# Where the operands of the rounded float32 products begin: large constants first in their pool, small tiles filled up

## The chip, the cores and the metric

The kernel runs on one core of a Trainium2 chip. The metric is the device time of one execution in microseconds (us): the median over several runs of the same program. TensorE (PE in the profile) does the matrix products, VectorE (DVE) and ScalarE (ACT) the elementwise work, GpSimd (POOL) a few small operations, and SyncE (SP) issues nearly all loads from device memory (HBM). Data are held in SBUF, 128 partitions with a byte address inside each; products land in PSUM, 8 banks per partition.

## The reference

Two layers, each an attention part and a feed-forward part, with a residual sum and a layer norm after each part. All inputs are float32. `x` is 2 x 512 tokens of width 512.

```python
x = layernorm(x + L0_attn(x))   # linear attention on a stored memory M, z; 8 key/value heads of 128
x = layernorm(x + L0_ffn(x))    # ternary weights; values truncated to int8 after up and after down
x = layernorm(x + L1_attn(x))   # one head of 128, softmax over 512 keys
x = layernorm(x + L1_ffn(x))    # silu(x Wg) * (x Wu), then Wd; inner width 1376
```

The inner width of both feed-forward parts is 1376: ten chunks of 128 and one of 96.

## The kernel before, in words

**Two kinds of product.** A full float32 product is one call in the program and two matmul records in the trace. A product of two tiles of type `float32r` (called rounded float32 here: the tile is written already rounded) is one record. The two attention parts use full float32: queries (line 334), the read of the memory (379), query/key (778), value (791), scores (806), attention times values (863), output (880). The two feed-forward parts use rounded products. Layer 0 up (line 539) multiplies ternary weights `tu` with a high and a low part of the rows, `xh` and `xl`, 352 products; layer 0 down (595) has 88. Layer 1 splits rows and weights each into three rounded parts and forms three products for each product of the reference: up (977) has 528, down (1052) has 231 of 512 columns and 66 of 256. In each product one tile is loaded into the array (the stationary operand, 128 or 96 columns a partition) and the other streams through (the moving operand, 512 columns, 256 in the 66).

**Order of the work.** The two batches `b` are worked side by side, in four stages: layer 0 attention, layer 0 feed-forward, layer 1 attention, layer 1 feed-forward. The order on each engine is that of the program, with some operations tied behind others by name; POOL's order is the written one alone. Loads go out on SP's queue in the written order, all weights of layer 0 first; those of layer 1 wait for the buffers of layer 0.

**Memory.** Tiles come from pools that lie one behind the other in each partition. Inside a pool the tags follow in the order of their first use, and each tile takes its bytes per partition rounded up to 32. The first pool, `const`, begins at byte 16512, which is 129 x 128. Its tags in order are `bq`, `z`, `ident`, four single columns, `ones`, `wqkv`, `bqk`, `bv`, `wo1`, `bo`, and small tables and flags. Then follow `wffn` (up weights, tags `gu0` to `gu10`), `xp` (the rows), `xtp` (two transposed row blocks, tag `xt`), `small` (columns of statistics, among them `col`, four buffers), `wop` (six pairs of rows, tag `wo`), `wqp` (four, tag `wq`), and the pools of the stages.

The space is used again under other names. The layer 0 high parts `xh` are `xt` tiles; the low parts `xl` are `wo` tiles; the ternary up weights `tu` are `wq` tiles; the ternary down weights `td` lie in `gu` tiles (line 583). In layer 1 the row parts of batch 0 (`r0_0` to `r0_5`, line 898) are `wo` tiles; those of batch 1 are two `xt` and two `wq` tiles (lines 902, 903). Weight parts take whatever units are free: `it_early` (stage pool), `ugu` (in `gu` tiles, line 746), `uwd` (in tiles of the down weights), `u_wqkv`, `u_wo1` and `u_bo` (in `const`, lines 1081 to 1083).

Where the pools and the operand tiles begin, as the rest of the byte address over 128:

| Place | Operands of rounded products there | Rest over 128 |
|---|---|---|
| `const`: wqkv | `u_wqkv` | 64 |
| `const`: wo1, bo | `u_wo1`, `u_bo` | 96 |
| `wffn` | `td`, `ugu` | 64 |
| `xtp` | `xh`, two tiles of the batch 1 row parts | 64 |
| `wop` | `xl`, row parts of batch 0 | 0 |
| `wqp` | `tu`, two tiles of the batch 1 row parts | 0 |
| stage pools | `it_f`, `it_early`, `uwd` | 0 |

By place, 369 of the 1199 products of 512 columns have both operands at a rest of 0. In 382 only the moving operand is at 64, in 257 only the stationary one; in 145 both are at 64; the other 46 have one at 96.

**Other places that the change touches.** The start: POOL builds the identity `ident` (line 86), DVE fills `ones` (96), and eight products of `ones` (101) run before the first transposes. `fold(h)` (line 363): one product, a column `c` of tag `col` written by ACT and read by ACT in the next operation; it is called for h = 0 and 1, 2 and 3, 4, 5 and 6, 7 at five points of the query loop.

Of the kernel before, what the change touches and what calls it, by code (L numbers as in the profile page):

```python
# [10 lines left out]
F32 = mybir.dt.float32  # L11
# [8 lines left out]
P = 128  # L20
B, S, HID = 2, 512, 512
NT = S // P
NK = HID // P
NH, G, D = 8, 4, 128
# [12 lines left out]
def kernel(  # L37
# [19 lines left out]
    nc = tc.nc  # L57
# [3 lines left out]
    const = ctx.enter_context(tc.tile_pool(name="const", bufs=1))  # L61
# [3 lines left out]
    small = ctx.enter_context(tc.tile_pool(name="small", bufs=4))  # L65
    ps = ctx.enter_context(tc.tile_pool(name="ps", bufs=8, space=PSUM))

    def psum(name):
        return ps.tile([P, 512], F32, tag="mm", name=name)

# [11 lines left out]
    bq = const.tile([D, NH], F32, tag="bq", name="bq")  # L82
    z = const.tile([D, NH], F32, tag="z", name="z")

    ident = const.tile([P, P], F32, tag="ident", name="ident")
    make_identity(nc, ident)
    ln_eps = const.tile([P, 1], F32, tag="ln_eps", name="ln_eps")
    nc.vector.memset(ln_eps, LN_EPS)
# [3 lines left out]
    nc.vector.memset(den_eps, DEN_EPS)  # L92
    below_half = const.tile([P, 1], F32, tag="below_half", name="below_half")
    nc.vector.memset(below_half, -BELOW_HALF)
    ones = const.tile([P, P], F32, tag="ones", name="ones")
    nc.vector.memset(ones, 1.0)


    rise = psum("rise")
    for _ in range(8):  # L100
        nc.tensor.matmul(rise[:, :P], ones, ones, start=True, stop=True)
# [4 lines left out]
    def transposed(rows, name, cuts=0):  # L106


        xt = xtp.tile([P, NK, S], F32, tag="xt", name=f"xt_{name}")
        pts = {}  # L110

        def turn(k, t, i=0):
            if (k, i) not in pts:
                pts[k, i] = psum(f"pt_{name}_{k}_{i}")
            nc.tensor.transpose(pts[k, i][:, ts(t, P)], rows[t][:, ts(k, P)], ident)

        def copy(k, at, i=0):
            move = nc.vector.tensor_copy if k % 2 else nc.scalar.copy
            copies.append(move(xt[:, k, at], pts[k, i][:, at]))

        if cuts:
            for i in range(cuts):
                for t in range(i * NT // cuts, (i + 1) * NT // cuts):
                    for k in range(NK):
                        turn(k, t, i)
                for k in range(NK):
                    copy(k, ts(i, S // cuts), i)
        else:
            for k in range(NK):
                for t in range(NT):  # L130
                    turn(k, t)
                copy(k, slice(0, S))
        return xt
# [51 lines left out]
    def over_partitions(mx, name):  # L185

        k = mx.shape[-1]
        pm = psum(f"pmx_{name}")
        nc.tensor.transpose(pm[:k, :P], mx, ident)
        top = small.tile([k, 1], F32, tag=f"top{k}", name=f"top_{name}", bufs=1)  # L190
        nc.vector.reduce_max(top, pm[:k, :P], AX.X)
        dg = small.tile([k, k], F32, tag=f"dg{k}", name=f"dg_{name}", bufs=1)
        nc.vector.tensor_scalar_mul(dg, ident[:k, :k], top)
        return dg
# [41 lines left out]
    def up_weights(gu_in, name, chunks=range(len(CHUNKS))):  # L236
        gus = []
        for c in chunks:
            i, n = CHUNKS[c]
            gu = wffn.tile([P, 2, NK, n], F32, tag=f"gu{c}", name=f"gu{name}_{c}")  # L240
            at = 2 * HID * i
            nc.sync.dma_start(
                gu.rearrange("p a k i -> p (a k i)"),
                gu_in[at : at + 2 * HID * n].rearrange("(p f) -> p f", p=P),
            )
            gus.append(gu)
        return gus
# [36 lines left out]
    with tc.tile_pool(name="a0w", bufs=1) as a0w, tc.tile_pool(name="a0", bufs=2) as a0:  # L284
# [23 lines left out]
            wos.append(halves)  # L308

        gus += up_weights(gu0_in, "0", range(1, len(CHUNKS)))  # L310
        wqkv = const.tile([P, NK, 3 * D], F32, tag="wqkv", name="wqkv")
        nc.sync.dma_start(wqkv, wqkv_in.rearrange("(k p) f -> p k f", p=P))
        bqk = const.tile([D, 3], F32, tag="bqk", name="bqk")
        nc.sync.dma_start(bqk, bqk_in)
        bv = const.tile([P, D], F32, tag="bv", name="bv")
        nc.sync.dma_start(bv, bv_in.to_broadcast([P, D]))
        wo1 = const.tile([D, HID], F32, tag="wo1", name="wo1")
        nc.sync.dma_start(wo1, wo1_in)
        bo = const.tile([P, HID], F32, tag="bo", name="bo")
        nc.sync.dma_start(bo, bo_in.to_broadcast([P, HID]))  # L320


# [40 lines left out]
        def fold(h):  # L363
            p = psum(f"pmw_{h}")
            nc.tensor.matmul(p, m[:, h, :], wos[h], start=True, stop=True)
            c = small.tile([P, 1], F32, tag="col", name=f"col_{h}")
            nc.scalar.mul(c, p[:, LAST:], -1.0)
            nc.scalar.activation(mw[:, h, :LAST], p[:, :LAST], AF.Identity, bias=c)

# [72 lines left out]
        for h in range(NH):  # L442
            queries(1, xt1, h)
            if h == 0:
                sum_weights(nc.vector, 4)
                sum_weights(nc.gpsimd, 5)
                fold(0)
                fold(1)
                mx_up = largest(
                    [gus[0][:, a].rearrange("p k i -> p (k i)") for a in range(2)], "up"  # L450
                )
            elif h == 1:
                top_up = over_partitions(mx_up, "up")
            elif h == 2:
                sc_up, inv_up = scales(top_up, "up")
                fold(2)
                fold(3)
                sum_weights(nc.vector, 6)
                sum_weights(nc.gpsimd, 7)
            elif h == 3:  # L460
                fold(4)
            elif h == 5:
                fold(5)
                fold(6)
            elif h == 6:
                fold(7)
            if h >= 3:
                for _ in range(3):
                    check_up(*checks.pop(0))
# [699 lines left out]
```

## Time and profile before

| Quantity | Value |
|---|---|
| Median of 3 runs | 481.14 us (481.09 to 482.33) |
| Profiled execution, whole | 481.89 us |
| Its span, first to last instruction | 479.7 us |
| Granted TensorE clock, mean | 0.997 |
| Busy: PE, DVE, ACT, POOL | 98%, 73%, 57%, 24% |
| Layer 0 feed-forward, PE | 130.6 to 236.6 us |
| Layer 1 feed-forward, PE | 288.4 to 473.9 us |

In a row of instructions, `pm<-r,it_early 128*128 128x512 f32 x144` means: PSUM tile pm, from moving tile r and stationary tile it_early, 144 records. Numbers in tile names are left out. Ends of matmuls are modelled and overlap; the time that a stream of matmuls takes is read from the starts of neighbouring rows. A row with several records (`x8`) covers them from the first start to the last end.

### The profile page before, as it was taken

To read this page: it belongs to the slowest core of one execution; us is meant where nothing else is said; L and a number is where in the kernel's file an instruction comes from. 1 tells how busy PE (TensorE), PEld (TensorE's weight loads), DVE (VectorE), ACT (ScalarE), POOL (GpSimd) and SP (SyncE) were. 2 spreads that over 40 slices of the span, in tenths; PEclk is the share of its full clock that TensorE was granted. 3 is DMA by queue.
4 is the path that set the end of the run, shared out by engine and by line. 5 is a ranking of instruction groups with operands and counts; after the bars stand their busy time and mean duration, and the time that the engine had idled before them with its cause. 6 is when DMAs were issued, how large, how long until landed. Compare 5 with 4: busy or idle time off the path is not lost.

```text
span 479.7 us, 5815 instructions
## 1 busy us (share of the span) xinstructions
PE 470.9 (98%) x1891; PEld 329.6 (69%) x1891; DVE 349.9 (73%) x689; ACT 272.5 (57%) x512; POOL 115.1 (24%) x146
## 2 busy tenths in 40 slices
PE   9999999999999999999999999999999999999995
PEld 8454444434487788787766567888788888888885
DVE  1345677677666586756979989997875778999852
ACT  3344899556666867546645834686753565434221
POOL 0344102666530392000464032000000000023211
PEclk9999999999999999999999999999999999999998
DMA  8999700000043001121390000000000000001011
GB/s 303 389 357 336 296 2 0 0 0 1 2 128 110 3 1 26 65 91 34 113 385 2 0 1 1 1 1 0 1 0 1 1 1 1 0 23 40 27 45 44
DMA packets 13748, 33.98 MB, mean 71 GB/s; under 512 B 1872, under 2 KB 2768, under 8 KB 13712
## 3 DMA queue, kind: packets, MB, share of 16 engines
q1 hardware_dynamic: 13280, 32.85, 19.0%
q10 hardware_dynamic: 432, 0.66, 0.4%
q8 instruction: 22, 0.36, 0.3%
q14 instruction: 14, 0.11, 0.1%
HBM read 31.40 MB, written 2.10 MB: 70 GB/s over the span
## 4 chain that ended last, share of the span: by engine, by line
PE 71%; ACT 7%; DVE 5%; issue 3%; POOL 1%; POOLq 0%; DVEq 0%; ACTq 0%
PE pm L977 17%; PE pg_f L539 9%; PE pc L977 9%; PE pu_f L539 9%; PE pdm L1052 7%; PE pd_f L595 4%; PE pdc L1052 4%; DVE x L401 4%; PE pqk L778 3%; PE po L379 2%; ACT y L392 2%; ACT t L411 2%; PE pv L791 1%; PE po L880 1%; PE pot L863 1%
## 5 line engine op out<-in xcount | busy, mean ns | idle before, releaser
L379 PE MATMUL po<-mw,q 128*128 128x512 f32 x128 | 57.1, 598 | 0.4 <-DVE mv_a L142 0.2
L334 PE MATMUL pq<-xt_a,wq 128*128 128x512 f32 (+1 forms) x136 | 56.4, 567 | 0.0
L148 POOL TENSOR_TENSOR rstd_f<-mv_f,ln_eps 128x1 f32<-128x1 f32 x15 | 4.7, 313 | 185.8 <-DVE mv_f L1063 132.1
L379 PEld LDWEIGHTS po<-mw,q 128*128 128x128 f32 x128 | 23.0, 189 | 32.2 <-issue 17.7
L334 PEld LDWEIGHTS pq<-xt_a,wq 128*128 128x128 f32 x136 | 25.5, 190 | 27.5 <-issue 25.5
L977 PE MATMUL pm<-r,it_early 128*128 128x512 f32 x144 | 37.8, 393 | 0.4 <-ACT r L718 0.4
L977 PE MATMUL pm<-r,ugu 128*128 128x512 f32 (+1 forms) x144 | 36.8, 393 | 0.0
L977 PEld LDWEIGHTS pm<-r,it_early 128*128 128x128 f32 x144 | 27.0, 188 | 6.7 <-ACT r L718 0.7
L401 DVE SCALAR_TENSOR_TENSOR x<-po,den,x 128x511 f32<-128x511 f32 x40 | 29.8, 745 | 1.9
L977 PEld LDWEIGHTS pm<-r,ugu 128*128 128x128 f32 (+1 forms) x144 | 26.8, 186 | 6.3
L170 ACT ACTIVATE ta_f<-y_f,below_half 128x512 int8<-128x512 f32 (+1 forms) x22 | 15.9, 722 | 24.4 <-DVE y_f L160 23.9
L988 DVE SCALAR_TENSOR_TENSOR ev_q<-pm,ev_q 128x512 f32<-128x512 f32 (+1 forms) x28 | 19.2, 687 | 14.0 <-PE pm L977 14.0
L396 POOL TENSOR_TENSOR y<-y,y 128x511 f32<-128x511 f32 x16 | 20.3, 1270 | 31.5 <-ACT y L392 30.8
L565 DVE SCALAR_TENSOR_TENSOR it_f<-tb_f,ta_f 128x512 fp32r<-128x512 int16 (+1 forms) x22 | 15.2, 690 | 16.0 <-ACT tb_f L171 15.9
L977 PE MATMUL pc<-r,ugu 128*128 128x512 f32 (+1 forms) x96 | 26.1, 394 | 0.0
L340 ACT ACTIVATE e<-pq,bq 128x512 f32<-128x512 f32 x16 | 11.1, 693 | 25.8 <-PE pq L334 25.8
L413 POOL TENSOR_SCALAR td<-wd,inv_down 128x512 fp32r<-128x512 f32 (+1 forms) x11 | 19.5, 1792 | 24.8 <-DVE inv_down L204 24.4
L539 PE MATMUL pg_f<-xh,tu 128*128 128x512 f32 (+1 forms) x88 | 25.1, 405 | 0.0
L539 PE MATMUL pu_f<-xh,tu 128*128 128x512 f32 (+1 forms) x88 | 24.0, 394 | 0.0
L539 PE MATMUL pg_f<-xl,tu 128*128 128x512 f32 (+1 forms) x88 | 23.9, 393 | 0.0
L539 PE MATMUL pu_f<-xl,tu 128*128 128x512 f32 (+1 forms) x88 | 23.9, 393 | 0.0
L987 ACT ACTIVATE ev_q<-pc 128x512 f32<-128x512 f32 (+1 forms) x28 | 16.4, 591 | 12.1 <-PE pc L977 12.1
(292 smaller groups left out, 1106.0 us busy)
## 6 DMA issues: line engine op xcount, KB each, us to landing
gu<-in_gu SPq DMA_DIRECT2D x20, 512.0 KB, 7.9
wo<-in_wo SPq DMA_DIRECT2D x16, 512.0 KB, 7.6
wd<-in_wd SPq DMA_DIRECT2D x20, 256.0 KB, 4.7
wq<-in_wq SPq DMA_DIRECT2D x8, 256.0 KB, 4.5
out<-x SPq DMA_DIRECT2D x7, 256.0 KB, 2.0
x<-in_x SPq DMA_DIRECT2D x6, 256.0 KB, 5.4
gu<-in_gu SPq DMA_DIRECT2D x2, 384.0 KB, 6.5
wqkv<-in_wqkv SPq DMA_DIRECT2D x1, 768.0 KB, 10.8
```

The lines of the kernel that those rows point to most:

```text
L170: nc.scalar.activation(a[:n], y, AF.Relu, bias=below_half[:n])
L334: nc.tensor.matmul(pq[:, at], wq[h][:, k, :], xt[:, k, at], start=(k == 0), stop=(k == NK - 1),)
L379: nc.tensor.matmul(po, qs[b][h0 + j][:, ts(t, P)], mw[:, h0 + j, :], start=True, stop=True,)
L396: nc.gpsimd.tensor_add(ys[0][:, :LAST], ys[0][:, :LAST], y[:, :LAST])
L401: steps.append(nc.vector.scalar_tensor_tensor(x[:, :LAST], four[j][:, :LAST], d, x[:, :LAST], ALU.mult, ALU.add))
L413: eng.tensor_scalar(out, w, factor, None, ALU.mult)
L539: nc.tensor.matmul(pp[a][:n], t[:, a, i % NK, :n], x2[b][i], start=(i == 0), stop=(i == 2 * NK - 1),)
L595: nc.tensor.matmul(pd, inter[b][c][:n, ts(t, P)], td[c][:n].bitcast(F32R), start=(c == 0), stop=(c == last),)
L977: nc.tensor.matmul(p[:n], w, x, start=(left[id(p)] == begun[id(p)]), stop=(left[id(p)] == 1))
L987: nc.scalar.activation(ev[:n], pc, AF.Copy, scale=CROSS)
L988: nc.vector.scalar_tensor_tensor(ev[:n], pm, MAIN, ev[:n], ALU.mult, ALU.add)
L1052: nc.tensor.matmul(p[:, :w], got[j // 4][1][kind][:n, j % 4], down_parts[j][kind][:, cols], start=(j == 0 and kind == kinds[0]), stop=(j = ...
```

## The change

Six tiles of `const` (`ident`, `ones`, `wqkv`, `bv`, `wo1`, `bo`) are declared first, in this order, ahead of all small ones; where they are filled stays as it was. They take 11776 bytes, 92 x 128. A new tile `fill` of 64 bytes follows; one element of it is set to zero by POOL, which is a new instruction ahead of the identity. The small tiles of `const` take 704 bytes, so the pool goes from 12480 to 12544 bytes, 98 x 128. The tag `col` gets two buffers in place of four, which takes 64 bytes from `small` (2112 to 2048). `wffn`, `xp` and `xtp` therefore move up by 64 bytes, and `wop` and everything behind it stay where they are. All operands of rounded products then begin at a rest of 0. No other instruction is added, removed or moved in the program's text.

```diff
+    ident = const.tile([P, P], F32, tag="ident", name="ident")
+    ones = const.tile([P, P], F32, tag="ones", name="ones")
+    wqkv = const.tile([P, NK, 3 * D], F32, tag="wqkv", name="wqkv")
+    bv = const.tile([P, D], F32, tag="bv", name="bv")
+    wo1 = const.tile([D, HID], F32, tag="wo1", name="wo1")
+    bo = const.tile([P, HID], F32, tag="bo", name="bo")
+    fill = const.tile([P, 16], F32, tag="fill", name="fill")
+    nc.gpsimd.memset(fill[0:1, 0:1], 0.0)
...
-    ident = const.tile([P, P], F32, tag="ident", name="ident")
     make_identity(nc, ident)
...
-    ones = const.tile([P, P], F32, tag="ones", name="ones")
     nc.vector.memset(ones, 1.0)
...
-        wqkv = const.tile([P, NK, 3 * D], F32, tag="wqkv", name="wqkv")
         nc.sync.dma_start(wqkv, wqkv_in.rearrange("(k p) f -> p k f", p=P))
...
-        bv = const.tile([P, D], F32, tag="bv", name="bv")
-        wo1 = const.tile([D, HID], F32, tag="wo1", name="wo1")
-        bo = const.tile([P, HID], F32, tag="bo", name="bo")
...
-            c = small.tile([P, 1], F32, tag="col", name=f"col_{h}")
+            c = small.tile([P, 1], F32, tag="col", name=f"col_{h}", bufs=2)
```

## The prediction

> **What bounds the kernel now.** I read the page's busy shares first, then PE's waits, then the order of PE's instructions in single stretches.
>
> ```profile
> span 479.7 us, 5815 instructions
> PE 470.9 (98%) x1891; PEld 329.6 (69%) x1891; DVE 349.9 (73%) x689; ACT 272.5 (57%) x512; POOL 115.1 (24%) x146
> PE rise L101 <- DVE ones L96: 1.2, 1, 1.2
> PE pqk L778 <- ACT xt_a L119: 1.0, 1, 1.0
> PE pm L977 <- ACT r L718: 0.4, 1, 0.4
> PE po L379 <- DVE mv_a L142: 0.2, 1, 0.2
> ```
>
> These four are all the waits that the view of PE's waits lists: 2.8 us. PE is the bound from 1.2 us to 473.9 us; the 5.8 us behind it are the last norm and store. A change that moves no work between engines can only act through PE's rate, or by making PE wait.
>
> So I looked at that rate. Busy time doesn't show it, since the ends of matmuls are modelled; the distance of starts does. Three stretches from the timeline of PE (start us, duration, row):
>
> ```profile
> 357.10 1.08 PE L977 MATMUL pc<-r,it_early 128*128 128x512 f32 x4
> 358.02 1.98 PE L977 MATMUL pm<-r,it_early 128*128 128x512 f32 x8
> 359.83 1.07 PE L977 MATMUL pc<-r,it_early 128*128 128x512 f32 x4
> 360.74 1.98 PE L977 MATMUL pm<-r,it_early 128*128 128x512 f32 x8
> 362.55 0.39 PE L977 MATMUL pc<-r,it_early 128*128 128x512 f32 x1
> ```
> ```profile
> 392.08 1.08 PE L977 MATMUL pm<-r,ugu 128*128 128x512 f32 x4
> ...
> 401.24 0.40 PE L977 MATMUL pc<-r,ugu 128*128 128x512 f32 x1
> ```
> ```profile
> 220.61 13.02 PE L595 MATMUL pd_f<-td,it_f 128*128 128x512 f32 x55
> 233.47 0.60 PE L115 MATMUL pt_a<-ident,x 128*128 128x128 f32 x4
> ```
>
> The first has both operands on a multiple of 128: 24 matmuls in 362.55 - 357.10 = 5.45 us, 227.1 ns each. The second has the stationary tile `ugu` at a rest of 64: 40 matmuls in 9.16 us, 229.0 ns. In the third the moving tile `td` is at 64: 55 in 12.86 us, 233.8 ns. All are 128 x 128 x 512 products at a granted clock of 1.00, with no wait in them. Shape and clock are equal; the place differs, and so does the time, by up to 3%.
>
> The same from all starts (each record laid to its call in the program, distances above 245 ns left out, 1185 remain): mean 230.1 with both at 0; 230.6 with the stationary at 64; 232.9 with the moving at 64; 231.6 with both at 64; 231.4 over all. The mean of the aligned is no better because their runs are short: after a run of other places the first eight or so still go 226, 236, 228, 233, and only then settle at 227, 226, 227. From the seventh on the aligned mean is 227.9 (81 matmuls). The longest aligned run, at 288.4, needed about 20. Full float32 products show no such effect: 429 ns with the moving tile at 0, 64 or 96.
>
> **What the Trainium skill says.** "SBUF — State Buffer", section Operand start alignment, allows any multiple of the element size and says of it: "This is about legality, not speed", with nothing timed; the trace above supplies times. "TensorE: Matmul & The Clock Gate", section "Wait — 56ns, not 53.3ns?", gives a start distance of N / 2.4 GHz + 2.5 ns, 215.8 at 512 columns. The full float32 records agree (429 = 2 x 213.3 + 2.5); rounded ones, at 227 to 234, have 11 to 18 ns more, so there is something for a place to act on. The same page's note on the peak-current limiter says that one busy core doesn't trip it; the granted clock of 1.00 in both feed-forward stages agrees.
>
> **The change part by part.**
>
> *Operands of rounded products.* All 1199 products of 512 columns get the place of the first stretch. Layer 1 up and down are one unbroken stream from 301.5 to 473.9, so one settling of some 20 matmuls is nearly all that is lost: I take 226.9 there. Layer 0 is cut by transposes and small products, so I take 228, the 227.9 of later matmuls in aligned runs. By line, with today's means of the undisturbed starts:
> - L977: 528 x (230.6 - 226.9) = 1.95 us
> - L1052: 231 x (231.8 - 226.9) = 1.13 us
> - L539: 352 x (231.8 - 228) = 1.34 us
> - L595: 88 x (233.6 - 228) = 0.49 us
>
> Together 4.9 us. No trace of before has a whole stage aligned, so the bounds matter. Settled everywhere at the best steady value, 226.7: 1199 x 4.7 = 5.6 us. Never settled, at the mean of today's short runs, 230.1: 1199 x 1.3 = 1.5 us. I take 4.9 since every aligned run of 24 or more settled.
>
> The 66 products of 256 columns start 118.3 ns apart today, none of them aligned; half the saving of a full one gives 66 x 2.3 = 0.15 us, between 0 and 0.3. The 64 records of the values (L791, moving `wqkv` and stationary `xt_a` both at 64) start 112 ns apart, transposes of the same width 109: up to 64 x 2.5 = 0.16 us, at least 0.
>
> *Constants first.* Order of allocation alone: no DMA is moved, and SP's queue is the same. `ident`, `bv`, `bo` and `x` feed transposes, DVE and POOL: DVE's L712 takes 0.68 us writing `it_early` (rest 0) and 0.68 to 0.69 writing `ugu` (rest 64), so nothing there, from -0.1 to +0.1 us.
>
> *The fill.* One POOL memset ahead of the identity; the four at the start take 0.10 us each and start 0.03 apart. The identity is ready at 1.29 us and first used at 4.52, after the products of `ones`, which wait for DVE. Cover: 3.2 us; without it the price would be 0.1 us.
>
> *`col` with two buffers.* Writer and reader are both ACT, in order, and at most two folds lie together; the next reuse is several us later (folds at 40.8, 49.9, 62.8). No new wait on another engine. If ACT did wait, it would be for its own Identity operation of the same kind as L340's (693 ns), and `mw` is first read at 72.3: hidden, at most 0.7 us without cover.
>
> *What is late next.* DVE could take the place of PE. It works without a pause from 399.37, after two pauses in which it waited for PE (2.06 and 1.33 us), and its last weight part is used 0.38 us after its end:
>
> ```profile
> 396.02 0.69 DVE L988 SCALAR_TENSOR_TENSOR ev<-pm,ev 128x512 f32<-128x512 f32 x1 [2.06 <-PE pm L977]
> ...
> 398.76 0.69 DVE L988 SCALAR_TENSOR_TENSOR ev_q<-pm,ev_q 128x512 f32<-128x512 f32 x1 [1.33 <-PE pm L977]
> ...
> 414.57 0.68 DVE L713 TENSOR_TENSOR uwd<-uwd,m_wd 128x512 fp32r<-128x512 f32 x1
> ```
> ```profile
> 415.63 0.40 PE L1052 MATMUL pdc<-uwd,ugu 128*128 128x512 f32 x1
> ```
>
> Up to 399 DVE follows PE, so PE's lead is handed on. From there to 415.6 PE gains another 70 x 4.5 ns = 0.3 us, just under the 0.38. I take off 0.4 us for this place and for resettling after it. The stores, norms and loads follow PE: DVE waits for PE, POOL or ACT at several points between 236 and 300, so layer 0's gain is not held up there.
>
> *Sum.* -4.9 - 0.15 - 0.16 + 0.4 = -4.8 us. The span goes from 479.7 to 474.9, and with the 2.2 us around it the profiled execution from 481.89 to 477.1. That execution lies 0.75 us above the median of the runs, 481.14, so the median should be 476.3 (-1.0%).
>
> **The rivals.** About 0.3% (1.44 us) is what a measurement of this kernel can tell from no change.
>
> *It never settles.* The aligned stream stays with the five-step pattern (224, 231, 236, 228, 233, mean 230.4) in which the run at 288.4 spent its first 20. For it: that run, and all groups of four in L539, at about 231. Against: the runs at 323.8 and 357.1 settled. Gain 1.5 + 0.3 = 1.8 us, 479.3.
>
> *DVE becomes the bound in layer 1.* From 299.6 to 311.9 and from 399.4 on DVE has no pause. For it: in 412 to 430 it is busy 16.89 of 17.60 us. Against: part d of the last row block is done at 309.75 and used at 311.82, and DVE pauses for PE between the two stretches. If most of layer 1's 3.1 us went, 2.2 us would stay: 478.9.
>
> *The rest isn't what acts.* Every tile at a rest of 64 or 96 lies below byte 105800, every one at 0 above 107900: place in the partition and rest can't be told apart in this trace. If the lower region itself is slow, nothing changes: 481.1. Against it: within that region, tiles at 96 (232.5 as stationary under a moving tile at 0) differ from those at 64 (230.6), though there are only 21.
>
> *Slower.* With the moving and the stationary tile both in the low region, the stream could lock into the steady slow pattern of `td` (233.6) in place of today's mixture. That is 1199 x (233.6 - 231.4) = +2.6 us, 483.8. It decides once the mean distance passes 231.4 + 1440 / 1199 = 232.6 ns. Against: the 145 products with both in the low region average 231.6 today.
>
> **How the numbers follow.** Forecast as worked out 0.62; never settles 0.15; DVE bound 0.10; no effect 0.08; slower 0.05. The predicted time is the first, 476.3. Its own range is 475.2 (226.7 throughout, nothing lost: 5.6 + 0.3) to 477.6. The 8-in-10 range runs from 475.0 over the next two cases to 479.9 and leaves out the last two (0.13) and thin tails. Faster by over 0.3%: the first, the third and 0.09 of the second, 0.81. Within 0.3%: 0.06 of the second and the fourth, 0.14. Slower: 0.05.
>
> **What would show it.** Right: the 55 matmuls of L595 take 12.5 us or less in place of 12.86; the 40 of `r,ugu` 9.07 in place of 9.16; the stretch from L977's restart to the last L1052 loses about 3 us and layer 0's about 1.9; PE's waits stay near 2.8 us. DVE as bound: a new PE wait for DVE at L1052 or L977. The rest not acting: L595 keeps 233 to 234 ns. The forecast fails most likely through the settling, which I infer from a few runs of 24 and more.

## The result, and the profile after

The changed kernel takes 477.74 us (median of 4 runs, 477.53 to 478.22) against 481.41 for the kernel before on the same chip; ratio 0.9922, 95% interval [0.9905, 0.9939]. It is 3.7 us faster, where 4.8 were forecast. In a second measurement the ratio was 0.9912 [0.9898, 0.9926].

The page's head and the view of PE's waits, of the changed kernel (its lines are numbered 5 to 9 higher):

```profile
span 475.7 us, 5816 instructions
PE 466.6 (98%) x1891; PEld 329.3 (69%) x1891; DVE 349.5 (73%) x689; ACT 272.3 (57%) x512; POOL 115.4 (24%) x147
PE rise L110 <- DVE ones L105: 1.2, 1, 1.2
PE pqk L783 <- ACT xt_a L128: 1.0, 1, 1.0
PE pm L982 <- ACT r L723: 0.4, 1, 0.4
PE po L384 <- DVE mv_a L151: 0.2, 1, 0.2
```

The span is 4.0 us shorter. PE has the same number of records and the same waits to the tenth, and its busy time fell by 4.3 us; DVE and ACT work as long as before, and POOL's one more instruction is the fill. The time came out of PE's own pace.

The pace is seen in the timeline of PE of the changed kernel (start, duration, row): layer 0 down, and a stretch of layer 1 up in which the stationary tile comes from the up weights and from the constants.

```profile
218.69 12.77 PE L600 MATMUL pd_f<-td,it_f 128*128 128x512 f32 x55
231.30 0.60 PE L124 MATMUL pt_a<-ident,x 128*128 128x128 f32 x4
```
```profile
374.13 1.07 PE L982 MATMUL pm<-r,ugu 128*128 128x512 f32 x4
375.03 1.07 PE L982 MATMUL pm<-r,u_wqkv 128*128 128x512 f32 x4
375.94 1.07 PE L982 MATMUL pc<-r,ugu 128*128 128x512 f32 x4
376.85 1.07 PE L982 MATMUL pm<-r,u_wo 128*128 128x512 f32 x4
377.75 1.07 PE L982 MATMUL pm<-r,u_bo 128*128 128x512 f32 x4
378.66 1.07 PE L982 MATMUL pc<-r,ugu 128*128 128x512 f32 x4
```

The 55 matmuls of layer 0 down take 12.61 us, 229.3 ns each, where they took 12.86 (233.8). The 20 from 374.13 to 378.66 take 4.53 us, 226.5 ns each. In the same way from all rounded products of 512 columns (from the start of each to the start of the next; distances above 245 ns left out):

| Mean distance of starts, ns | Before | After |
|---|---|---|
| Layer 0 up (L539, now L544) | 231.8 | 227.8 |
| Layer 0 down (L595, now L600) | 233.6 | 229.2 |
| Layer 1 up (L977, now L982) | 230.6 | 227.5 |
| Layer 1 down (L1052, now L1057) | 231.8 | 229.3 |
| All | 231.4 | 228.1 |

### The profile page after: what moved, and what is told of

Read it like the earlier page. It is cut to its first block, busy times and chain, and to the rows that moved or that the text cites. A ratio compares the mean times of both kernels' runs of the same rounds, so it can differ in the third digit from the quotient of the medians.

```text
span 475.7 us, 5816 instructions
## 1 busy us (share of the span) xinstructions
PE 466.6 (98%) x1891; PEld 329.3 (69%) x1891; DVE 349.5 (73%) x689; ACT 272.3 (57%) x512; POOL 115.4 (24%) x147
## 4 chain that ended last, share of the span: by engine, by line
PE 71%; ACT 8%; DVE 5%; issue 3%; POOL 1%; POOLq 0%; DVEq 0%; ACTq 0%
PE pm L982 17%; PE pg_f L544 9%; PE pc L982 8%; PE pu_f L544 8%; PE pdm L1057 7%; PE pd_f L600 4%; PE pdc L1057 4%; DVE x L406 4%; PE pqk L783 3%; PE po L384 2%; ACT y L397 2%; ACT t L416 2%; PE pv L796 2%; PE po L885 1%; PE pot L868 1%
## 5 line engine op out<-in xcount | busy, mean ns | idle before, releaser
L982 PE MATMUL pm<-r,it_early 128*128 128x512 f32 x144 | 37.4, 390 | 0.4 <-ACT r L723 0.4
L982 PE MATMUL pm<-r,ugu 128*128 128x512 f32 (+1 forms) x144 | 36.3, 389 | 0.0
L982 PEld LDWEIGHTS pm<-r,it_early 128*128 128x128 f32 x144 | 27.0, 188 | 6.2 <-ACT r L723 0.7
L982 PEld LDWEIGHTS pm<-r,ugu 128*128 128x128 f32 (+1 forms) x144 | 26.8, 186 | 5.9
L982 PE MATMUL pc<-r,ugu 128*128 128x512 f32 (+1 forms) x96 | 25.8, 390 | 0.0
L544 PE MATMUL pg_f<-xh,tu 128*128 128x512 f32 (+1 forms) x88 | 24.8, 402 | 0.0
L544 PE MATMUL pg_f<-xl,tu 128*128 128x512 f32 (+1 forms) x88 | 23.6, 390 | 0.0
L544 PE MATMUL pu_f<-xh,tu 128*128 128x512 f32 (+1 forms) x88 | 23.6, 390 | 0.0
L544 PE MATMUL pu_f<-xl,tu 128*128 128x512 f32 (+1 forms) x88 | 23.6, 390 | 0.0
```

What stands on the lines that cost most here:

```text
L544: nc.tensor.matmul(pp[a][:n], t[:, a, i % NK, :n], x2[b][i], start=(i == 0), stop=(i == 2 * NK - 1),)
L982: nc.tensor.matmul(p[:n], w, x, start=(left[id(p)] == begun[id(p)]), stop=(left[id(p)] == 1))
```

## Experiments

The forecast read the trace as: a moving or stationary operand off a multiple of 128 costs time. The first four runs move the pools by 32 or 64 bytes to see whether the multiple is the cause, or that the two operands agree, or the region of the partition. "Lower pools" are those from `const` to `xtp`, "upper pools" `wop` and all behind it.

**Everything at 64.** One more tile in front of the constants of the changed kernel moves every pool by 64 bytes.

```diff
+    lead = const.tile([P, 16], F32, tag="lead", name="lead")
+    nc.gpsimd.memset(lead[0:1, 0:1], 0.0)
     ident = const.tile([P, P], F32, tag="ident", name="ident")
```

> The changed kernel with a tile of 64 bytes in front of its constants, so that every operand of a rounded product begins at a rest of 64 over 128 instead of 0. One more small POOL memset at the start. Theory A (a multiple of 128 is what counts, whichever the other operand): the stream no longer settles at 227 ns; the mean distance of starts returns to 231.5 (what pairs with both at 64 had before) or more, 1199 x 3.4 = 4.1 us, 481.8 us; layer 0 down at 231 to 234 ns. Theory B (moving and stationary must have the same rest, whichever): as the changed kernel, 477.7 us, mean distance 228, layer 0 down at 229 ns.

Measured: 477.47 us, ratio 0.9905 [0.9889, 0.9922]; mean distance 228.1. Its layer 0 down in the timeline of PE:

```profile
219.02 12.77 PE L602 MATMUL pd_f<-td,it_f 128*128 128x512 f32 x55
231.63 0.60 PE L126 MATMUL pt_a<-ident,x 128*128 128x128 f32 x4
```

12.61 us again, with no operand at a multiple of 128. The multiple is not the cause.

**Everything at 32.** The same with a tile of 32 bytes.

```diff
+    lead = const.tile([P, 8], F32, tag="lead", name="lead")
+    nc.gpsimd.memset(lead[0:1, 0:1], 0.0)
     ident = const.tile([P, P], F32, tag="ident", name="ident")
```

> The changed kernel with a tile of 32 bytes in front of its constants: every operand at a rest of 32 over 128. Theory A (multiples of 128): slow like a rest of 64, mean distance 231 to 234 ns, 481 to 484 us. Theory B (same rest): 477.7 us. Theory C (multiples of 64 would be enough once all are alike): all at 64 is fast, 477.7, and this one is slow, 481 or more.

Measured: 477.99 us, ratio 0.9917 [0.9900, 0.9933]; mean distance 228.1. Not even multiples of 64 are needed.

**The mirror image.** The column tag gets its four buffers back, so that the lower pools stay at 0 and the upper ones go to 64.

```diff
-            c = small.tile([P, 1], F32, tag="col", name=f"col_{h}", bufs=2)
+            c = small.tile([P, 1], F32, tag="col", name=f"col_{h}")
```

> The changed kernel with the column buffers back at four: the lower pools (constants, up weights, transposed rows) stay at a rest of 0, everything from the pair tiles on goes to 64. The mirror image of the kernel before. Theory A: moving xl and r0 are now off (about 680 products at 232.5 ns), the others have only the stationary operand off (229 to 230.6): mean 231.5, 481.8 us; layer 0 down, moving at 0 and stationary at 64, about 229. If the region of the partition were the cause and not the rest, no change from the changed kernel: 477.7 us, layer 0 down at 229 as well, layer 1 up of batch 0 still at 227.

Measured: 481.97 us, ratio 1.0000 [0.9991, 1.0009]: the whole gain is gone. Mean distance 231.4. Layer 0 down, where now the moving `td` is at 0 and the stationary `it_f` at 64:

```profile
220.44 13.02 PE L600 MATMUL pd_f<-td,it_f 128*128 128x512 f32 x55
233.30 0.60 PE L124 MATMUL pt_a<-ident,x 128*128 128x128 f32 x4
```

12.86 us, as in the kernel before, where it was the moving operand that stood at 64. The lower region isn't slow in itself, and neither operand alone decides. By the expectation it would have been about 229; that was wrong too, and the next runs say why.

**Only the transposed rows moved.** The fill goes from the constants to the pool of the rows, so that the up weights' tiles stay at 64.

```diff
-    fill = const.tile([P, 16], F32, tag="fill", name="fill")
+    fill = xp.tile([P, 16], F32, tag="fill", name="fill", bufs=1)
```

> The changed kernel with the 64 fill bytes moved from the constants' pool to that of the rows: transposed rows (xh, half of the row parts of batch 1) and constants at 0, the up weights' tiles (td, ugu) back at 64. Theory A, by line against the kernel before: layer 0 up fully aligned, -1.4 us; layer 0 down as before, 233.6 ns; layer 1 up, all moving at 0, stationary partly 64: -0.8; layer 1 down -0.1. Sum -2.3, 479.1 us. If the moving operand alone mattered: layer 1 up as in the changed kernel (227.5 ns).

Measured: 479.16 us, ratio 0.9945 [0.9928, 0.9961]. Layer 0 up has 227.8 ns as in the changed kernel, layer 0 down 233.8 as before, layer 1 up 228.8, layer 1 down 231.9. Each product follows its own two operands, and the parts add up; by the moving operand alone layer 1 up would have had 227.5.

**Agreement modulo what?** Modulo 128, +64 and -64 are the same. In the traces so far they aren't. Take the byte address of the stationary operand minus that of the moving one, modulo 256, and call neighbouring products of 128 rows, 128 columns and the same difference a run. From the seventh matmul of a run on, the distance is 233.3 ns at a difference of 64, and 229 at -64. The mirror image, too, was none over 256: in the kernel before, `wffn` and `xtp` lie at 64 and the upper pools at 128; in the mirror image these are 128 and 192. In both the upper pools are 64 ahead, and both kernels take the same time. So the next run keeps every operand at a multiple of 128, but moves the lower pools against the upper ones by 128; the pool of statistics gives up the bytes, so that the upper pools stay.

```diff
+    lead = const.tile([P, 32], F32, tag="lead", name="lead")
+    nc.gpsimd.memset(lead[0:1, 0:1], 0.0)
     ident = const.tile([P, P], F32, tag="ident", name="ident")
...
+    pad = small.tile([P, 16], F32, tag="pad", name="pad", bufs=1)
+    nc.gpsimd.memset(pad[0:1, 0:1], 0.0)
...
-        st = small.tile([P, cuts, 6], F32, tag=f"st{cuts}", name=f"st_{b}_{t}")
+        st = small.tile([P, cuts, 6], F32, tag=f"st{cuts}", name=f"st_{b}_{t}", bufs=1 if cuts > 1 else 4)
```

> The changed kernel with 128 bytes in front of the constants and 128 bytes less in the pool of statistics: every operand still begins at a multiple of 128, but the lower pools lie at a rest of 0 over 256 and the upper ones at 128. From the runs so far the rest itself doesn't count, only whether the two operands agree. Theory B128 (they must agree modulo 128): as the changed kernel, 477.7 us, layer 0 down at 229 ns. Theory B256 (they must agree modulo 256 or more): slow again, 481 to 483 us, layer 0 down at 231 ns or more, though every operand is at a multiple of 128.

Measured: 481.80 us, ratio 1.0006 [0.9997, 1.0014]; mean distance 231.6; layer 0 down:

```profile
221.38 12.98 PE L604 MATMUL pd_f<-td,it_f 128*128 128x512 f32 x55
234.20 0.60 PE L128 MATMUL pt_a<-ident,x 128*128 128x128 f32 x4
```

12.82 us. This kernel does what the change says, all operands begin at multiples of 128, and it gains nothing. What has to agree is the place modulo 256. That 256 is enough is in the changed kernel's stretch above: `u_wqkv`, `u_wo1` and `u_bo` lie at 128 over 512, the moving rows at 384, and they run at 227.

**Other differences.** The lower pools 32 and 96 bytes ahead of the upper ones. The diff is that of 32; for 96 both new tiles have 24 columns, and the pool of statistics gives up its bytes at `st`, as in the run before.

```diff
+    lead = const.tile([P, 8], F32, tag="lead", name="lead")
+    nc.gpsimd.memset(lead[0:1, 0:1], 0.0)
...
+    pad = small.tile([P, 8], F32, tag="pad", name="pad", bufs=1)
+    nc.gpsimd.memset(pad[0:1, 0:1], 0.0)
...
-        sums = small.tile([P, NT], F32, tag="sums", name=f"sums_{b}")
+        sums = small.tile([P, NT], F32, tag="sums", name=f"sums_{b}", bufs=2)
```

> Lower pools 32 bytes ahead of the upper ones (rests over 256: 160 and 128). Stationary minus moving is -32 in layer 0 down and +32 in layer 1 up of batch 0 where the weights lie in up-weight tiles. At a difference of +64 the steady distance was 233.3 ns, at -64 it was 229, at 0 it was 226.7. If any difference costs: 228 to 234 in both, about 480 to 482 us; if only differences of 64 or more cost, 477.7.

> Lower pools 96 bytes ahead of the upper ones (rests over 256: 224 and 128): differences -96 in layer 0 down, +96 in layer 1 up of batch 0 on up-weight tiles. If what counts is the place over 128, -96 is +32 and +96 is -32, and the two distances are those of the run with 32 exchanged; if it is the place over 256, they are new values. Whole: 480 to 483 us by either.

Measured: 481.89 us (ratio 1.0008 [0.9998, 1.0017]) and 482.61 us (1.0025 [1.0013, 1.0037]; a little slower than the kernel before). From the seventh matmul of a run on:

| Stationary minus moving, modulo 256 | Distance of starts, ns | Read from |
|---|---|---|
| 0 | 227.0 | changed kernel, 902 matmuls |
| +32, -32 | 233.3, 233.4 | rel32: layer 1 up; layer 0 down |
| +64, -64 | 233.3, 228.9 | before: layer 0 down; layer 1 up |
| +96, -96 | 234.3, 234.0 | rel96: layer 1 up; layer 0 down |
| 128 | 232.7 | rel128, both |

The two signs stem mostly from different products, but that doesn't explain why -64 costs only a third of the others: within layer 1 up of the kernel before, 74 matmuls at -64 take 228.9 and 8 at +64 take 233.2. The reason stays open.

**What breaks the pace in the changed kernel.** Distances of starts in its layer 1 down, first row block, from its first product on (a star: 96 rows in the contraction, the last chunk):

```
227 226 227 227 232* 238 232 231 227 226 227 227 226 226 248
226 227 227 226 233* 236* 233 233 236 224 231 236 228 233 231 226 227 227
```

After each product of 96 rows some three to ten matmuls pass until 227 is back. The next kernel fills the contraction up to 128 rows with zeros in both down products.

```diff
+            if n < P and name == "1":
+                nc.gpsimd.memset(wd[n:], 0.0)
             nc.sync.dma_start(wd[:n], wd_in[i : i + n, :])
...
-        weight_parts(wds[c][:n], parts, f"wd{c}")
-        down_parts.append([u[:n] for u in parts])
+        weight_parts(wds[c], parts, f"wd{c}")
+        down_parts.append(parts)
...
-                            p[:, :w], got[j // 4][1][kind][:n, j % 4], down_parts[j][kind][:, cols],
+                            p[:, :w], got[j // 4][1][kind][:, j % 4], down_parts[j][kind][:, cols],
...
         its = inter_tiles("f0", F32R)
+        for b in range(B):
+            nc.gpsimd.memset(its[b][2][96:, 2, :].bitcast(F32), 0.0)
...
+            if n < P:
+                nc.gpsimd.memset(td[c][n:], 0.0)
...
-                        pd, inter[b][c][:n, ts(t, P)], td[c][:n].bitcast(F32R),
+                        pd, inter[b][c][:, ts(t, P)], td[c].bitcast(F32R),
```

> The changed kernel with the last chunk's contraction of 96 rows filled up to 128 by rows of zeros in both down products (same columns streamed, same result; four small POOL memsets more). In the changed kernel the six to nine matmuls after each of 96 rows start 231 to 238 ns apart before 227 comes back. If the 96 rows are what breaks the pace: layer 0 down from 229.2 to 227.2 (-0.2 us), layer 1 down from 229.3 to 227 (-0.5 us), sum -0.7 us, 477.0. If it is the change of accumulation bank at the same place: no change, 477.7.

Measured: 476.54 us, ratio 0.9897 [0.9881, 0.9914]. Layer 0 down falls to 227.3 ns, layer 1 down to 226.7: 226 of its 231 distances are 225 to 227. Layer 0 down in the timeline:

```profile
218.51 12.65 PE L606 MATMUL pd_f<-td,it_f 128*128 128x512 f32 x55
231.00 0.60 PE L124 MATMUL pt_a<-ident,x 128*128 128x128 f32 x4
```

12.49 us, 227.1 ns each. The accumulation bank changes at the same places as before, so the 96 rows were the break. By the trace that is 88 x 1.9 + 231 x 2.6 ns = 0.8 us; the interval of the ratio overlaps that of the changed kernel, so the distances show the step, not the time.

**The changed kernel again**, beside the last two.

> The changed kernel itself, beside the two that follow, for a ratio on the same chip: 477.7 us, ratio to the kernel before 0.992.

Measured: 477.22 us, 0.9912 [0.9898, 0.9926]; distances as in the table above to 0.2 ns.

**The 96-column tiles of layer 1 up** are laid at a stride of 128 columns.

```diff
+        if n == NK * 96:
+            h, l, d = (u.rearrange("p (k i) -> p k i", k=NK)[:, :, :96] for u in parts)
+            w, m, big = (u.rearrange("p (k i) -> p k i", k=NK) for u in (w, m, big))
...
-        h, l, d = (u[:, : NK * n].rearrange("p (k i) -> p k i", k=NK) for u in up_parts[j, a])
+        h, l, d = (u.rearrange("p (k i) -> p k i", k=NK)[:, :, :n] for u in up_parts[j, a])
```

> The changed kernel, with the 96-column weight parts of the last chunk of layer 1 up laid at a stride of 128 columns (512 bytes) in place of 96 (384 bytes): same products, no padding. At a stride of 384 bytes every second block differs from its moving operand by 128 modulo 256, and the 48 products start 233.3 ns apart; in layer 0 the same width at a stride of 512 starts 230.5 apart. If agreement modulo 256 is the rule: 230.5 here too, 48 x 2.8 = -0.13 us (too small for the times, readable in the trace). If the width of 96 alone makes 233: no change.

Measured: 477.53 us, 0.9918 [0.9903, 0.9933], no difference in time, as expected for so small a part. The 48 products go from 233.1 to 230.1 ns (232, 228, 229, 231 in turn), like those of layer 0. In the changed kernel every second block had been 128 off its partner, and the blocks between were slow with them (233.7 and 232.5). So agreement counts inside a tile too, and the width of 96 costs some 3 ns of its own.

**All products of one shape.** rows128, and the 96-column tiles of both up products filled up to 128 columns with zeros.

```diff
             ts_up[c] = t.rearrange("p a (k i) -> p a k i", k=NK)
+            if n < P:
+                nc.gpsimd.memset(ts_up[c][:, :, :, n:].bitcast(F32), 0.0)
...
-                            pp[a][:n], t[:, a, i % NK, :n], x2[b][i],
+                            pp[a], t[:, a, i % NK], x2[b][i],
...
+            for u in wide:
+                nc.gpsimd.memset(u[:, :, 96:].bitcast(F32), 0.0)
...
-        h, l, d = (u[:, : NK * n].rearrange("p (k i) -> p k i", k=NK) for u in up_parts[j, a])
+        h, l, d = (u.rearrange("p (k i) -> p k i", k=NK) for u in up_parts[j, a])
...
```

> rows128 with the 96-column stationary tiles of both up products filled up to 128 columns of zeros as well (POOL memsets; the upper 32 rows of the PSUM results are not read). If every matmul then has the same shape and the operands agree: 227 ns through the whole of layer 1, L982's mean from 227.5 to 227.0, layer 0 up from 227.7 to 227.4; -0.4 us against rows128, so 476.1 us, -1.6 against the changed kernel. Rival: the wider weight load or the memsets on POOL cost something, and it is not below rows128 (476.5).

Measured: 475.95 us, ratio 0.9884 [0.9867, 0.9901]. Layer 1 up has 226.9 ns, layer 1 down 226.8, layer 0 up and down 227.3; mean 227.05. This is the fastest of all: 1.3 us below the changed kernel on the same chip. The two intervals just meet, and the distances say the same: 1199 x (228.1 - 227.05) ns = 1.3 us. Against rows128, on another chip, its median is 0.6 us lower with intervals that overlap widely; that step shows in the distances alone.

## Why the forecast came out, and where it was wrong

**PE is the bound, and the change acts through its pace.** Right: no wait in the view of PE's waits changed, and the span lost what the distances lost.

**The cause.** The observation was right (same shape, same clock, 227 to 234 ns by the place of the operands), and so was the step that the changed operands get the place of the first stretch. The reading behind it was wrong. "A multiple of 128" isn't what counts: everything at 64 or at 32 is as fast, and everything at multiples of 128 with a shift of 128 is as slow as before. What counts is that the moving and the stationary operand agree modulo 256. The trace of before could have shown half of it. In it every long run of agreeing pairs stood at 0. The 145 pairs with both at 64 say little against that place: nearly all lie in runs of at most six, and the first six of the runs at 0 average 230.8, the pairs at 64 231.6. That a moving operand at 64 looked worse than a stationary one (232.9 against 230.6 in the prediction) was the sign of the difference: the first is +64, the second nearly always -64, and the 12 products with the stationary operand at 64 and a difference of +64 took 233.8. That the change works was in part luck: it brings agreement modulo 256 by the sizes of its pools, while its own rule would allow 128, and a layout that keeps that rule, rel128, gains nothing.

**The sum, term by term.**

| Term | Forecast, us | Measured, from the distances |
|---|---|---|
| Layer 1 up | 1.95 | 528 x 3.1 = 1.6 |
| Layer 1 down | 1.13 | 231 x 2.5 = 0.6 |
| Layer 0 up | 1.34 | 352 x 4.1 = 1.4 |
| Layer 0 down | 0.49 | 88 x 4.4 = 0.4 |
| 66 products of 256 columns | 0.15 | -0.1: from 118.8 to 119.9 ns |
| Values (64 records) | 0.16 | 0: still 112 ns |
| Lost to DVE and resettling | -0.4 | -0.02 |
| Sum | 4.8 | 3.9 |

Part of the nearness is cancellation: the 0.4 us taken off for DVE, which cost 0.02, made up for as much of what the gains were overrated.

The mis-sized term is the pace in layer 1, taken as 226.9 ns in one unbroken stream. The stream has no wait, but it has breaks: the chunk of 96 rows in each of layer 1 down's groups (229.3 in place of 226.9; with 128 rows 226.7), and 48 products with 96 columns in layer 1 up (233.1). The stretch from layer 1 up's restart to its last product, which was to lose about 3 us, lost 2.1: from 172.1 to 170.0 us.

```profile
301.52 1.18 PE L977 MATMUL pc<-r,ugu 128*128 128x512 f32 x4
473.63 0.28 PE L1052 MATMUL pdm<-uwd,ugu 128*128 128x256 f32 x1
```
```profile
299.38 1.16 PE L982 MATMUL pc<-r,ugu 128*128 128x512 f32 x4
469.36 0.28 PE L1057 MATMUL pdm<-uwd,ugu 128*128 128x256 f32 x1
```

Layer 0 down was missed for the same reason: its 55 matmuls took 12.61 us, where 12.5 or less was to be the sign, and came to 12.49 only with the 96 rows filled up. The two small gains didn't come. The products of 256 columns became 1 ns slower (all 65 distances of before average 118.8; the prediction read 118.3). The values' 112 ns stayed, as by the true rule it had to: their two operands, both at 64 before, agreed already.

**The DVE stretch.** The margin there did shrink as worked out. The last weight part of DVE and its use on PE in the changed kernel, from the two timelines, and the weight load of that product (PEld), before and after:

```profile
410.95 0.69 DVE L718 TENSOR_TENSOR uwd<-uwd,m_wd 128x512 fp32r<-128x512 f32 x1
```
```profile
411.78 0.41 PE L1057 MATMUL pdc<-uwd,ugu 128*128 128x512 f32 x1
```
```profile
415.40 0.19 PEld L1052 LDWEIGHTS pdc<-uwd,ugu 128*128 128x128 f32 x1
```
```profile
411.69 0.19 PEld L1057 LDWEIGHTS pdc<-uwd,ugu 128*128 128x128 f32 x1 [0.17 <-DVE uwd L718]
```

The 0.38 us from DVE's end to the use on PE became 0.14, and nothing is left of the margin. The weight load, which comes first, now sits idle for 0.17 us until DVE is done, and the next matmul starts 248 ns after this one, some 20 ns late (47 ns in rows128). That is too small for the view of PE's waits. The danger was seen rightly and its price was mis-sized: the 0.4 us taken off were hardly needed. A further gain of PE just ahead of this point would be lost here.

**The rivals.** "It never settles" fell: the 902 matmuls that are seventh or later in an aligned run average 227.0. "The rest isn't what acts" fell in its form, the region, through the mirror image; its doubt about the rest was sound. "Slower" didn't occur in the changed kernel; rel96 shows that such a layout exists, though at a ratio of only 1.0025 to the kernel before.

**The fill, `col`, the constants.** Nothing: POOL's instruction is hidden, and no wait of ACT or PE came with the two buffers.

## What to carry to other kernels

Where PE is the bound and its products are rounded float32, look at the distance of starts in a stream without waits, by the byte addresses of both operands; the share of busy time, 98% before and after, hides the loss. Lay the moving and the stationary operand at the same place modulo 256 bytes, whichever it is, and keep every block inside a tile there too. Then look for the odd shapes: an edge chunk of 96 filled up to 128 costs no streamed column and here gave another 1.3 us by the distances.

## What the runs showed of the hardware

- Rounded products of 512 columns start 226.5 to 227 ns apart at best in these runs, at a granted clock of 1.00; once a stream has settled, a difference of the two operands (stationary minus moving) of 32 or 96 either way, of 128 or of +64 bytes modulo 256 makes it 233 to 234, one of -64 some 229.
- The pace has memory: after a product of another shape or a transpose, up to some ten matmuls go 224 to 238 before 227 is back (over twenty at the start of layer 1 up, at 286 us). What in PE agrees or disagrees wasn't tried, nor whether it is the operand of the same or of the next product that counts.
- Full float32 products don't care: the records of the queries start 429 ns apart whether their operands agree (changed kernel) or lie 64 (before) or 128 bytes apart (rel128).
- Rounded products of 256 columns are the exception: 119.9 ns in the layouts in which all operands agree, 118 to 119 in the mixed ones.
